# First layer of a selective-scan network: a new plan of the pieces in a round

## The chip, the cores and the metric

The kernel runs on one core of one Trainium2 chip. The metric is the device time of the whole kernel in microseconds; lower is better. A core has five engines that run at the same time, each with its own queue of instructions in a fixed order: TensorE (PE in the profile, matrix products; PEld its weight loads), VectorE (DVE), ScalarE (ACT), GpSimd (POOL) and SyncE (SP), which here issues almost all DMA transfers. An engine that reaches an instruction whose inputs aren't ready waits, and everything behind that instruction in its queue waits with it.

## The reference

Two layers work on an image x of 4 x 64 x 64 x 192. Only the first matters here. It normalizes x, projects it to 384 channels, and runs a selective scan over the 4096 positions in four directions k (by rows, by columns, and both backwards):

```python
delta = softplus(delta + delta_bias)          # one step size per channel and position
def step(h, inp):
    dt, ut, bt, ct = inp
    dA = exp(dt[..., None] * A_k[None])       # A has the 16 values -1 .. -16 for each channel
    dBu = dt[..., None] * bt[:, :, None, :] * ut[..., None]
    h = dA * h + dBu
    y = einsum('bkdn,bkn->bkd', h, ct)        # sum over the 16 states n
    return (h, y)
```

The four results are put back into image order and summed, normalized, gated, projected to 192 channels and added to x.

## The kernel before

The scan is not run position by position. `FirstLayer.scans` cuts the 4096 positions into 137 rounds of 30 positions. In a round the four directions and four images are handled together, with two blocks of positions on the 128 partitions, and the 16 states n are worked through one after another: a round is 16 **steps**, and step s of the program (`for s in range(-LEAD, N + 8)`, line 1094 on) belongs to round s // 16. The decays are exponentials of sums of dt inside the round, and since the sixteen values of A are whole multiples of one, the tile x of one state follows from the one before by one multiplication with a common factor f.

In every step, by its line in the profile:

- `grown` (L1073, on the first state of a round L1069) makes x for a later step: POOL multiplies 1024 of the 1536 columns, DVE the other 512. POOL is six steps ahead (`AHEAD = 6`), DVE five. On the first state DVE reads the exponentials that `first_near` (L916) put into the PSUM tile p.
- `carry_in` (L1024, two DMAs) puts the state that earlier rounds left into eight rows of x. It is issued three steps ahead of the use.
- `mix` (L1079) is the product on PE, in two halves j, each 8 matmuls into the accumulator accs[j] in PSUM. `weigh` (L1090, DVE, one for each half) multiplies the accumulator by fd; in the last step of a round `end_y` (L962) does so into the output tile y.
- In odd steps ACT copies the accumulators before they are weighed (`keep_end`, L1029, two halves). From that copy and from `decay` (L1039, ACT) and `settle` (L1042, POOL) comes the state for the next round, which SP moves (L1016 small, L1045 carry).
- In even steps PE makes the outer products of b and c for two later states (`outer`, L1053) and DVE cuts them out with a mask (`cut_b`, L1061).

Around this the preparation of the next rounds is threaded in pieces. `Round.steps` is a plan written out by hand: each entry is a step, counted from the round's first, an engine, and a piece. The pieces are: `v` (L845, a product on PE), `parts` (L862 and L863, ACT), `exp` (L867, ACT), `plus` (L871, ACT), `rounded` (L875, POOL), `log` (L878, ACT), eight `delta` products (L845, PE) that together give softplus, `times_u` (L890, DVE), `keep_dt` (L895, ACT); then sums of dt on PE, `sums_far` (L899), `sums_near` (L913) and `sums_d` (L845), and their exponentials on ACT: `first_far` and `fall_far` (L904, L909), `first_near` and `fall_near` (L916, L920), `keep_sums` (L929, which gives fd); and the sixteen `spread` pieces (L837, ACT), which make the weights of `outer`. All these products go through one single PSUM tile, p: a new product waits until the last reader of the one before is done. Three more `sums_d(0)` in the plan compute what nobody reads.

`keep_total` (DMA, L1016), `log_total` (L937, ACT) and `test` (L940, DVE) guard the range: `test` takes a running minimum into `far`, a corner of the second bank of accs[1], in columns that the products don't use.

Inside a step the program emits the work in the order of the loop: SP's, then ACT's copies, `decay`, the planned ACT pieces, POOL's, then DVE's `weigh`, `grown`, `cut_b`, the planned DVE pieces, then PE's `mix` for the next step, the planned PE pieces, and `outer`. Each engine keeps that order. Waits between engines are set by a tracker of tiles; nothing reorders.

Of the kernel before, what the change touches and what calls it, by code (L numbers as in the profile page):

```python
# [14 lines left out]
NB, HW, CH = 4, 64, 192  # L15
# [15 lines left out]
PART = 4  # L31
# [547 lines left out]
class FirstLayer(Stage):  # L579
# [182 lines left out]
    def scans(self):  # L762
        nc, tc = self.tc.nc, self.tc
        with ExitStack() as ctx:
            pool = lambda name, bufs, **k: ctx.enter_context(tc.tile_pool(name=name, bufs=bufs, **k))
# [43 lines left out]
            class Round:  # L809
# [164 lines left out]
                def steps(self):  # L974

                    s = lambda f, *a: (lambda: f(*a))
                    r = [(-30, "sp", self.load_xd), (-20, "sp", self.load_u), (-12, "sp", self.load_bc)]
                    for i in range(NS // PART):
                        r += [(PART * i - 8 + b, "act", s(self.spread, i, b)) for b in range(NB)]
                    for j in range(2):  # L980
                        r += [(2 * j - 21, "pe", s(self.v, j)), (2 * j - 20, "act", s(self.parts, j))]
                        r += [(2 * j - 19, "act", s(self.exp, j))]
                        r += [(2 * j - 13, "dve", s(self.times_u, j)), (2 * j - 13, "act", s(self.keep_dt, j))]
                        r += [(2 * j - 10, "pe", s(self.sums_d, j)), (2 * j - 9, "act", s(self.keep_sums, j))]
                    r += [(at, "pe", s(self.delta, 0, i)) for i, at in enumerate((-17, -16, -15, -14))]
                    r += [(at, "pe", s(self.delta, 1, i)) for i, at in enumerate((-13, -13, -12, -12))]
                    r += [(-16, "act", self.plus), (-15, "pool", self.rounded), (-14, "act", self.log)]
                    for i, at in ((1, -10), (2, -8)):
                        r += [(at - 1, "pe", s(self.sums_far, i))]
                        r += [(at, "act", s(self.first_far, i)), (at, "act", s(self.fall_far, i))]  # L990
                    r += [(-6, "pe", self.sums_near), (-5, "act", self.first_near), (-5, "act", self.fall_near)]
                    r += [(-4, "sp", self.keep_total), (-2, "act", self.log_total), (-1, "dve", self.test)]
                    r += [(10, "sp", self.load_y), (NS + 5, "pool", self.add_old), (NS + 6, "sp", self.store_y)]
                    r += [(at, "pe", s(self.sums_d, 0)) for at in (-7, -4, -2)]
                    return r

            w_dt, one, shift, zeros, late = self.w_dt, self.one, self.shift, self.zeros, self.late
# [2 lines left out]
            AHEAD = 6  # L1000
# [7 lines left out]
            def planned(s, engine):  # L1008
                for f in plan.get((s, engine), []):
                    f()  # L1010
# [7 lines left out]
            def carry_in(s):  # L1018
                n = state(s)
                m = (n - 1) // 2  # L1020
                v = carry[:, n % 2, m : m + 2].rearrange("c m q r f -> r (m q) c f")
                for r in range(2):
                    to = xs[s][r * HALF + 2 * RW : (r + 1) * HALF].rearrange("q (c f) -> q c f", c=2)
                    nc.sync.dma_start(to, v[r])  # L1024

            def keep_end(s, j):
                if j == 0:
                    sxs[s] = p3.tile([128, W], F32, name="sx")
                nc.scalar.copy(paired(sxs[s], j), accs[j][:, :, :DI])  # L1029

            def shrink(s):
                small[s] = p3.tile([128, SMALL], F32, name="small")
                for c in range(2):
                    narrow(small[s], sxs[s], c)

            def decay(s):
                back[s] = p3.tile([128, SMALL], F32, name="back")
                n = state(s)
                nc.scalar.activation(back[s], of(s).tot, AF.Exp, bias=late[:, n // 2 : n // 2 + 1], scale=float(n))  # L1039

            def settle(s):
                nc.gpsimd.tensor_tensor(back[s], back[s], small[s], ALU.mult)  # L1042

            def carry_out(s):
                nc.sync.dma_start(carry_of(carry, (state(s) - 1) // 2), back[s])  # L1045

            def outer(s):
                outs[s] = ps_o.tile([128, LC], F32, name="o")
                cs, p = of(s).cs[s % NS // PART], of(s).r % 2
                for h in range(2):  # L1050
                    n = state(s) - 1 - h
                    at = slice(h * NB * HALF, (h + 1) * NB * HALF)
                    nc.tensor.matmul(  # L1053
                        outs[s][:, at], at_b[p][:, n, :], cs[:, n % PART].rearrange("q b l -> q (b l)"),
                        start=True, stop=True, skip_group_check=True,
                    )

            def cut_b(s):
                bs[s] = p_b.tile([128, 2, NB, HALF], F32, name="b")
                o = outs[s].rearrange("p (h b l) -> p h b l", h=2, b=NB)  # L1060
                nc.vector.tensor_tensor(bs[s], o, bc(masks, 2, NB), ALU.mult)  # L1061

            def grown(s, engine):
                it = of(s)
                if s not in xs:
                    xs[s] = p_x.tile([128, W], F32, name="x")
                if s % NS == 0:
                    part, g = (slice(0, LC), it.m[:, 1, :]) if engine is nc.vector else (slice(LC, W), it.g)
                    engine.tensor_tensor(xs[s][:, part], it.dtu[:, part], g, ALU.mult)  # L1069
                    return  # L1070
                part = slice(0, LC) if engine is nc.vector else slice(LC, W)
                f = it.f0 if engine is nc.vector else it.f
                engine.tensor_tensor(xs[s][:, part], xs[s - 1][:, part], f, ALU.mult)  # L1073

            def mix(s, j):
                for r in range(2):
                    for c in range(2):
                        b = 2 * c + j
                        nc.tensor.matmul(  # L1079
                            accs[j][half(c), r, :DI], bs[s - s % 2][half(r), s % 2, b, :], xs[s][half(r), cols(b)],  # L1080
                            start=s % NS == 0, stop=state(s) == 1, skip_group_check=True,
                        )

            def weigh(s, j):
                n = state(s)
                if n == 1:
                    of(s).end_y(j)
                    return
                acc = accs[j][:, :, :DI]
                nc.vector.tensor_tensor(acc, acc, paired(of(s).fd, j), ALU.mult)  # L1090

            engines = {e.engine for e in (nc.tensor, nc.scalar, nc.vector, nc.gpsimd, nc.sync)}
            with tc.manual_schedule(engines=engines):
                tc.keep_in_program_order(nc.scalar.preload_act_table_set("natural_log_exp_and_others"))
                for s in range(-LEAD, N + 8):
                    on = lambda q: 0 <= q < N
                    pair = lambda q: on(q) and state(q) % 2 == 1
                    if pair(s - 1):
                        shrink(s - 1)
                    if pair(s - 5):  # L1100
                        carry_out(s - 5)
                    if on(s + AHEAD - 3):
                        carry_in(s + AHEAD - 3)
                    planned(s, "sp")
                    if pair(s):
                        for j in range(2):
                            keep_end(s, j)
                    if pair(s - 2):
                        decay(s - 2)
                    planned(s, "act")  # L1110
                    if on(s + AHEAD):
                        grown(s + AHEAD, nc.gpsimd)
                    if pair(s - 4):
                        settle(s - 4)
                    planned(s, "pool")
                    if on(s):
                        for j in range(2):
                            weigh(s, j)
                    if on(s + AHEAD - 1):
                        grown(s + AHEAD - 1, nc.vector)  # L1120
                    if on(s + 2) and s % 2 == 0:
                        cut_b(s + 2)
                    planned(s, "dve")
                    for j in range(2):
                        if on(s + 1):
                            mix(s + 1, j)
                    planned(s, "pe")
                    if on(s + 4) and s % 2 == 0:
                        outer(s + 4)
# [719 lines left out]
```

## Time and profile before

| what | us |
|---|---|
| median of 3 runs (9069.08 to 9072.87) | 9069.21 |
| the profiled execution, its own time | 9073.65 |
| its span | 9071.8 |
| scans of the first layer in it, about | 690 to 7320 |
| PE busy | 8250.5 (91%) |
| DVE busy | 7532.0 (83%) |
| POOL busy | 6608.1 (73%) |
| ACT busy | 6053.4 (67%) |

Times in the text are microseconds. A profile row of the timeline gives the start, the duration, the engine, the line, the operation, the tiles it writes and reads, the shape, and how many such instructions in a row were joined; in brackets stands how long the engine had idled before it and what ended that ("issue" where the profile shows no cause). DVE and ACT instructions overlap a little: a weighing lasts 0.96, but the next instruction starts 0.87 after it. A row of the waits gives who waited, for what, then the us in total, how many times, and the longest.

### The profile page before, as it was taken

What the parts mean: (1) busy time and instruction counts of PE and PEld (TensorE: products, weight loads), DVE (VectorE), ACT (ScalarE), POOL (GpSimd) and SP (SyncE); (2) the same over time, 40 slices, a digit from 0 to 9 for tenths busy, and PEclk for the clock granted to TensorE, in tenths of its full rate; (3) what the DMA queues carried; (4) which work ended last, traced back from release to release, by engine and by line L of the source; (5) the groups of instructions that cost most, each with busy time, mean ns of one, the idle gap of its engine ahead of it and who ended that gap; (6) DMA issues with size and microseconds to landing.
All of it is one profiled execution on the core that took longest, in us unless ns stands there. A gap on an engine that the chain in (4) does not pass through costs nothing. (4 is left out here: it accounts for less than half of the span.)

```text
span 9071.8 us, 194263 instructions
## 1 busy us (share of the span) xinstructions
PE 8250.5 (91%) x64280; PEld 3615.7 (40%) x64280; DVE 7532.0 (83%) x10238; ACT 6053.4 (67%) x10104; POOL 6608.1 (73%) x3814
## 2 busy tenths in 40 slices
PE   8989999999999999999999999999999945786668
PEld 4433333333333333333333333333333335443457
DVE  3328999999999999989999999999999954796756
ACT  3336777777777777766776777777677745575658
POOL 0008999999999999999999999999999942001460
PEclk9999999999999999999999999999999977887789
DMA  6652333323333333233333333333333379343558
GB/s 186 211 183 65 75 76 75 78 75 76 75 79 75 75 76 78 73 76 83 82 83 81 83 83 86 81 82 84 82 80 85 82 204 255 111 137 119 163 134 294
DMA packets 952264, 971.21 MB, mean 107 GB/s; under 512 B 550175, under 2 KB 802732, under 8 KB 950368
## 3 DMA queue, kind: packets, MB, share of 16 engines
q1 hardware_dynamic: 946192, 951.97, 38.6%
q0 software_dynamic: 5056, 6.66, 0.5%
q8 instruction: 519, 8.50, 0.4%
q14 instruction: 497, 4.07, 0.1%
HBM read 521.83 MB, written 375.80 MB: 99 GB/s over the span
## 5 line engine op out<-in xcount | busy, mean ns | idle before, releaser
L1073 POOL TENSOR_TENSOR x<-x,f 128x1024 f32<-128x1024 f32 x2055 | 4865.3, 2368 | 412.4 <-PE acc L1079 102.9
L1090 DVE TENSOR_TENSOR acc<-acc,fd 128x768 f32<-128x768 f32 x4110 | 3763.7, 959 | 272.2 <-ACT sx L1029 232.9
L1079 PE MATMUL acc<-x,b 64*64 64x384 f32 x35072 | 3502.3, 501 | 104.8 <-DVE acc L940 49.3
L1029 ACT COPY sx<-acc 128x768 f32<-128x768 f32 x2192 | 1669.0, 807 | 1011.9 <-PE acc L1079 910.5
L1079 PEld LDWEIGHTS acc<-x,b 64*64 64x64 f32 x35072 | 1075.1, 132 | 2100.3 <-DVE acc L1090 1577.0
L1073 DVE TENSOR_TENSOR x<-x,f 128x512 f32<-128x512 f32 x2055 | 1391.6, 677 | 0.1
L1053 PE MATMUL o<-cs,at_b 8*128 8x256 f32 x4384 | 1235.6, 400 | 2.4 <-DVE b L1061 2.4
L837 ACT ACTIVATE cs<-at_c,own 8x256 f32<-8x256 f32 x2192 | 1069.0, 494 | 2.8 <-PE o L1053 2.7
L1053 PEld LDWEIGHTS o<-cs,at_b 8*128 8x128 f32 x4384 | 726.9, 184 | 750.2 <-issue 269.3
L1061 DVE TENSOR_TENSOR b<-o,masks_f 128x512 f32<-128x512 f32 x1096 | 749.1, 683 | 4.7 <-PE o L1053 4.7
L462 PE MATMUL pp<-xT,w_in 96*128 96x512 f32 x1536 | 713.8, 616 | 20.9 <-ACT pad L1286 20.3
L875 POOL TENSOR_SCALAR d<-l 128x1536 f32<-128x1536 f32 x137 | 201.6, 1471 | 668.9 <-ACT l L871 668.9
L845 PE MATMUL p<-dt,steps_f 64*64 64x384 f32 x5480 | 598.1, 505 | 43.2 <-ACT up L863 25.5
L904 ACT ACTIVATE g<-p,shift 128x512 f32<-128x512 f32 x274 | 188.3, 687 | 492.7 <-PE p L899 492.7
L1300 DVE SCALAR_TENSOR_TENSOR acc<-pad,conv_w_s,acc 128x2048 f32<-128x2048 f32 x192 | 440.7, 2344 | 47.7 <-ACT acc L1298 46.4
L965 POOL TENSOR_TENSOR yt<-yt,yold 128x1536 f32<-128x1536 f32 x137 | 471.7, 3443 | 0.0
L462 PEld LDWEIGHTS pp<-xT,w_in 96*128 96x128 f32 x1536 | 291.9, 197 | 369.7 <-issue 340.9
L1042 POOL TENSOR_TENSOR back<-back,small 128x96 f32<-128x96 f32 x1096 | 424.3, 387 | 15.4 <-DMA small<-sx 6.4
L1039 ACT ACTIVATE back<-tot,late_f 128x96 f32<-128x96 f32 x1096 | 431.3, 394 | 0.0
L862 ACT ACTIVATE e<-p 128x768 f32<-128x768 f32 x274 | 221.5, 808 | 286.5 <-PE p L845 268.9
L549 PE MATMUL op<-w_out,v 128*128 128x192 f32 x1536 | 286.5, 344 | 132.2 <-DVE ot L552 96.4
L1281 POOL MEMSET pad<- 128x66 f32 x12 | 1.9, 158 | 554.5 <-DVE acc L1300 491.1
(218 smaller groups left out, 9650.9 us busy)
## 6 DMA issues: line engine op xcount, KB each, us to landing
x<-carry SPq DMA_DIRECT2D x4384, 24.0 KB
ut<-uT SPq DMA_DIRECT2D x548, 180.0 KB
small<-sx SPq DMA_DIRECT2D x2192, 24.0 KB
carry<-back SPq DMA_DIRECT2D x1096, 48.0 KB
zg<-gate SPq DMA_DIRECT2D x64, 768.0 KB
yold<-y_row SPq DMA_DIRECT2D x546, 90.0 KB
y_row<-yt SPq DMA_DIRECT2D x546, 90.0 KB
y_col<-yt SPq DMA_DIRECT2D x546, 90.0 KB
```

Of the source, the lines that this page charges most:

```text
L462: self.tc.nc.tensor.matmul(pp, self.w_in[:, i, e * 128 : (e + 1) * 128], self.xT[:, i, t * LC : (t + 1) * LC], start=(i == 0), stop=(i == ...
L837: nc.scalar.mul(self.cs[part][:, :, b, :], at_c[self.r % 2][:, at : at + PART, :], own[:, b : b + 1])
L845: nc.tensor.matmul(self.m[half(b), a, :DI], w(a, 2 * b + j), t(a, 2 * b + j), start=start and n == 0, stop=stop and n == len(terms) - 1, s ...
L965: nc.gpsimd.tensor_tensor(self.y, self.y, yold, ALU.add)
L1029: nc.scalar.copy(paired(sxs[s], j), accs[j][:, :, :DI])
L1039: nc.scalar.activation(back[s], of(s).tot, AF.Exp, bias=late[:, n // 2 : n // 2 + 1], scale=float(n))
L1053: nc.tensor.matmul(outs[s][:, at], at_b[p][:, n, :], cs[:, n % PART].rearrange("q b l -> q (b l)"), start=True, stop=True, skip_group_chec ...
L1061: nc.vector.tensor_tensor(bs[s], o, bc(masks, 2, NB), ALU.mult)
L1073: engine.tensor_tensor(xs[s][:, part], xs[s - 1][:, part], f, ALU.mult)
L1079: nc.tensor.matmul(accs[j][half(c), r, :DI], bs[s - s % 2][half(r), s % 2, b, :], xs[s][half(r), cols(b)], start=s % NS == 0, stop=state(s ...
L1090: nc.vector.tensor_tensor(acc, acc, paired(of(s).fd, j), ALU.mult)
L1300: nc.vector.scalar_tensor_tensor(acc, part(tap), weight(tap), acc, ALU.mult, ALU.add)
```

## The change

The entries of the plan get other steps. `v`, `parts`, `exp`, `plus`, `rounded` and `log` move one step earlier. The sums are reordered: `sums_d` now in steps 5 and 7 of the round before (counted 0 to 15), `sums_far` in steps 6 and 8, `sums_near` in step 9. Their ACT pieces follow: `keep_sums` in steps 6 and 8, `first_far` and `fall_far` in steps 7 and 9, `first_near` and `fall_near` in step 10. The spreads go in pairs into even steps. The three unread products move to steps 11, 13 and 14.

In the loop, `carry_in` is issued four steps ahead instead of three; DVE's `grown` is six steps ahead like POOL's; the planned ACT pieces come before `decay`; and `test` has a place of its own, ahead of the step's `weigh` and `end_y`.

```diff
                     for i in range(NS // PART):
-                        r += [(PART * i - 8 + b, "act", s(self.spread, i, b)) for b in range(NB)]
+                        r += [(PART * i - 8 + b // 2 * 2, "act", s(self.spread, i, b)) for b in range(NB)]
                     for j in range(2):
-                        r += [(2 * j - 21, "pe", s(self.v, j)), (2 * j - 20, "act", s(self.parts, j))]
-                        r += [(2 * j - 19, "act", s(self.exp, j))]
+                        r += [(2 * j - 22, "pe", s(self.v, j)), (2 * j - 21, "act", s(self.parts, j))]
+                        r += [(2 * j - 20, "act", s(self.exp, j))]
                         r += [(2 * j - 13, "dve", s(self.times_u, j)), (2 * j - 13, "act", s(self.keep_dt, j))]
-                        r += [(2 * j - 10, "pe", s(self.sums_d, j)), (2 * j - 9, "act", s(self.keep_sums, j))]
+                        r += [(2 * j - 11, "pe", s(self.sums_d, j)), (2 * j - 10, "act", s(self.keep_sums, j))]
+                        r += [(2 * j - 10, "pe", s(self.sums_far, j + 1))]
+                        r += [(2 * j - 9, "act", s(f, j + 1)) for f in (self.first_far, self.fall_far)]
...
-                    r += [(-16, "act", self.plus), (-15, "pool", self.rounded), (-14, "act", self.log)]
-                    for i, at in ((1, -10), (2, -8)):
-                        r += [(at - 1, "pe", s(self.sums_far, i))]
-                        r += [(at, "act", s(self.first_far, i)), (at, "act", s(self.fall_far, i))]
-                    r += [(-6, "pe", self.sums_near), (-5, "act", self.first_near), (-5, "act", self.fall_near)]
-                    r += [(-4, "sp", self.keep_total), (-2, "act", self.log_total), (-1, "dve", self.test)]
+                    r += [(-17, "act", self.plus), (-16, "pool", self.rounded), (-15, "act", self.log)]
+                    r += [(-7, "pe", self.sums_near), (-6, "act", self.first_near), (-6, "act", self.fall_near)]
+                    r += [(-4, "sp", self.keep_total), (-2, "act", self.log_total), (-1, "sum", self.test)]
...
-                    r += [(at, "pe", s(self.sums_d, 0)) for at in (-7, -4, -2)]
+                    r += [(at, "pe", s(self.sums_d, 0)) for at in (-5, -3, -2)]
...
-                    if on(s + AHEAD - 3):
-                        carry_in(s + AHEAD - 3)
+                    if on(s + AHEAD - 2):
+                        carry_in(s + AHEAD - 2)
                     planned(s, "sp")
                     if pair(s):
                         for j in range(2):
                             keep_end(s, j)
+                    planned(s, "act")
                     if pair(s - 2):
                         decay(s - 2)
-                    planned(s, "act")
...
                     planned(s, "pool")
+                    planned(s, "sum")
                     if on(s):
                         for j in range(2):
                             weigh(s, j)
-                    if on(s + AHEAD - 1):
-                        grown(s + AHEAD - 1, nc.vector)
+                    if on(s + AHEAD):
+                        grown(s + AHEAD, nc.vector)
```

## The prediction

> **What bounds the kernel now.** First the page's 40 slices and two stretches, to find the stage; then the timeline of one clean round, engine by engine; then the waits.
>
> ```profile
> span 9071.8 us, 194263 instructions
> PE   8989999999999999999999999999999945786668
> DVE  3328999999999999989999999999999954796756
> POOL 0008999999999999999999999999999942001460
> ```
>
> ```profile
> 690.00:7320.00 6630.00, 6409.77 (x56622) 2467.34 (x56618) 6124.69 (x8085) 4703.91 (x8066) 6189.72 (x3565) 0.99 0.32 79
> 2338.33:2385.93 47.60, 46.51 (x414) 17.62 (x414) 44.66 (x60) 34.42 (x60) 45.18 (x26) 1.00 0.31 76
> ```
>
> (Columns: length, then busy us of PE, weight loads, DVE, ACT, POOL; granted clock.) The change touches the scans alone: 6630 of 9072 us, 137 rounds of 16 steps. The second row is one clean round of 47.60: PE 46.5, POOL 45.2, DVE 44.7. Three engines are nearly full, so no single one is "the" bound; a round is lost in small waits between them. From the first L962 (758.2) to the last (7306.0) lie 136 rounds, 48.1 each: besides the clean 47.6 there is about 0.55 of disturbance.
>
> ```profile
> 2359.85 1.83 DVE L1090 TENSOR_TENSOR acc<-acc,fd 128x768 f32<-128x768 f32 x2 [0.41 <-ACT sx L1029]
> 2365.69 1.83 DVE L1090 TENSOR_TENSOR acc<-acc,fd 128x768 f32<-128x768 f32 x2 [0.49 <-ACT sx L1029]
> 2373.62 0.69 DVE L1069 TENSOR_TENSOR x<-dtu,p 128x512 f32<-128x512 f32 x1 [0.85 <-issue]
> 2377.54 1.83 DVE L1090 TENSOR_TENSOR acc<-acc,fd 128x768 f32<-128x768 f32 x2 [0.30 <-ACT sx L1029]
> 2383.43 1.82 DVE L962 TENSOR_TENSOR yt<-acc,fd 128x768 f32<-128x768 f32 x2 [0.55 <-ACT sx L1029]
> 2385.77 0.26 DVE L940 TENSOR_TENSOR acc<-acc,tot 128x96 f32<-128x96 f32 x1
> ```
>
> These are steps 7, 9, 11, 13, 15: DVE waits for ACT's copies (L1029) or for ACT's exponentials. Packed, DVE repeats at 0.87 (weighing), 0.60 (growth), 0.60 (cut), 0.17 (test): 44.0 a round, so 3.6 are waits. ACT and PE, same round:
>
> ```profile
> 2364.29 0.68 ACT L909 ACTIVATE f<-p,shift 128x512 f32<-128x512 f32 x1
> 2364.86 1.50 ACT L1029 COPY sx<-acc 128x768 f32<-128x768 f32 x2
> 2372.87 0.66 ACT L920 ACTIVATE f<-p,shift 128x512 f32<-128x512 f32 x1
> ```
>
> ```profile
> 2362.54 1.12 PE L899 MATMUL p<-dt,steps_f 128*128 128x512 f32 x2
> 2363.59 1.52 PE L1079 MATMUL acc<-x,b 64*64 64x384 f32 x16
> 2365.02 0.88 PE L845 MATMUL p<-dt,steps_f 64*64 64x384 f32 x8
> 2365.82 1.12 PE L1053 MATMUL o<-cs,at_b 8*128 8x256 f32 x4
> 2366.88 1.57 PE L1079 MATMUL acc<-x,b 64*64 64x384 f32 x16
> 2386.08 0.88 PE L1079 MATMUL acc<-x,b 64*64 64x384 f32 x8 [0.58 <-DVE acc L940]
> ```
>
> The copies of step 9 stand right behind L909; PE runs without a gap from 2362.54 to 2366.88. Its pitches: both products 1.43, L845 0.80, L899 or L913 1.05, L1053 1.06.
>
> ```profile
> PEld acc L1079 <- DVE acc L940: 135.9, 135, 1.3
> ACT tot L937 <- DMA tot<-fd: 79.8, 70, 2.4
> PE acc L1079 <- DMA x<-carry: 41.4, 71, 6.4
> ```
>
> **Steps of the reckoning.** From the timeline: first weighing to the next step's product 1.03 (2371.0 to 2372.0 and alike); product to copy 0.89, copy to weighing 0.84, product to weighing without a copy 0.95; L899's start to its exponential 1.16. I lay the changed plan out with these, in us after the round's first weighing (before: read off):
>
> start of step 2, 5, 6, 8, 10, 11, 12, 14, next 0
> before: 5.56, 14.89, 18.09, 23.85, 29.69, 32.62, 35.89, 41.54, 47.60
> after: 5.34, 14.68, 17.87, 23.60, 29.43, 33.69, 36.04, 41.59, 47.81
>
> How the second row comes: step 1's second product starts at 0.87 + 1.03 = 1.90, then delta and L1053 end at 4.40, + 0.94 = 5.34. Step 5: two delta products wait for times_u (start 10.60, + 0.95 + 0.06), 1.34 long, then 0.89 + 0.84. Step 6: + 3.19, DVE packed with times_u. Step 8 and 11: (a), (b). Step 10: step 9's second product at 25.59, + 0.78 + 1.06 + 1.05 = 28.48, + 0.95. Step 12: v(0) at 33.23, + 0.80 + 1.06 + 0.95. Step 14: step 13's second product at 38.03, + 0.75 + 0.80 + 1.06 + 0.95. Next 0: L962 at 45.48 (d), + 0.87 + 0.86 + 0.60.
>
> **Part by part.**
> (a) *Far exponentials to odd steps, sums between.* Step 6 now gives ACT only keep_sums (0.78) ahead of the copies, not two of 0.59 behind a longer product. The 0.49 at step 7 goes (17.87 + 2.93 = 20.80). But L899 (1.05) now shares the even step with L1053 (1.06): the second product of step 7 starts at 19.77, + 0.75 + 1.05 + 1.06 = 22.65 before step 8's product may start, + 0.95 = 23.60 where DVE would be ready at 23.13. The same again at step 10. What ACT gives, PE's queue takes: steps 6 to 10 last 11.56 against 11.60. Gain 0.04.
> (b) *Near sums, and DVE's growth one step earlier.* L1069 waited for L920, not merely for L916, which it reads: it starts 0.09 after L920's end (2373.53), 1.06 after L916's. Now L913 follows step 10's products: 28.48 + 1.43 = 29.91; L916 at +1.16, L920 +0.66, L1069 at 32.48. DVE is ready at 29.43 + 1.73 = 31.17: 1.31 lost against 0.85-0.95 before, because L1069 moved forward as well. Behind it stand the cut and step 11's weighing; on PE, v(0) waits for the buffer and L1053 behind v(0). Steps 10 to 12: 6.61 against 6.20, loss 0.41.
> (c) *v, parts, exp one step earlier.* In step 14 ACT keeps exp (0.73) instead of parts (1.40), in step 12 exp instead of parts: the 0.30 at step 13 nearly goes, PE holds back 0.1 and 0.19. Steps 12 to 14: 5.55 against 5.65, gain 0.10. Plus (1.45, ahead of a decay) falls into step 15 behind copies, with 2 us till the next; rounded then fills POOL's idle time at the round's start. No cost; without that cover, 1.45.
> (d) *Test ahead of the products of y.* The test writes accs[1]. L940 held step 0's second product, though that product touches other columns (0.58 above); that goes. But in front of L962 the test must wait for what reads accs[1] before it: the second copy. Page "PSUM — Partial Sum Buffer", section "PSUM bank collisions raise a hardware error": guard by bank and quadrant, not by address. By addresses the test would cost 0.17, and the round end at 47.02; by the rule it waits until 44.47 + 0.84 = 45.31 and L962 starts at 45.48, not 44.69: 0.79. The row (products held by a test in other columns) sides with the rule, so I take 0.79. Behind the test stand both L962, the growth, step 0's weighing; PE's products and so POOL wait for these. Step 14 to the following round's step 1: 9.15 against 9.27, gain 0.12, where (c) alone would have brought 0.6.
> (e) Steps 0 to 6 otherwise: loss 0.06 (step 1 without its former slack, step 4 to 5 as before: the two delta products behind times_u).
> Sum: +0.04 +0.10 +0.12 -0.41 -0.06 = -0.21 a round, 29 us slower in 137.
> (f) *Spreads in pairs*: as many, in even steps, where ACT idles; 0. Decay behind the planned work: settle on POOL reads it two steps later; 0 to 0.1. The spare products stay three; the clock stays 1.00.
> (g) *Carry transfers a step earlier.* 32 DMAs a round pass, in SP's queue, the loads and stores of their step: y stores (8 of about 0.42, step 6), y loads (step 10). Product 11, which waits for them, is later in about a fourth of the rounds: in the mean of all rounds step 10 lasts 0.28 more than in a clean one (weighing starts, timeline). One step is 3 us, and (b)'s stall covers 1 us more: I take it all, -0.28; at least nothing, as the transfer also waits for growth, POOL's included, one step nearer.
> (h) *Late totals* (second half; y loads are then twice as many): step 14 and 15 last 0.25 and 0.26 more there. The first stays (exp, copies and test stand behind L937 as parts did). The second goes: the spare product of step 14 no longer waits for parts. Over all rounds -0.13, at least 0.
> Together +0.21 - 0.28 - 0.13 = -0.20 a round, 27 us. The profiled run is 9073.65 against a median of 9069.2; the difference is taken off the median: about **9043**.
>
> **Rivals.**
> 1. *Gains add up* (0.12): the test doesn't wait for the copies, or PE's queue yields in (a). For: every DVE wait of the timeline names ACT, which is relieved. Against: rows above. With the test free -0.79 more: 9043 - 108 = **8935**.
> 2. *SP's queue takes it back* (0.28), the slower side. Carry_in now needs POOL's growth of the step before. In step 7 that ends at 2359.7 (after add_old), DVE's at 2358.9: SP is held 0.8, with the small transfers, y loads and totals behind. In the second half SP issues almost without a pause, so the 0.8 reaches L937, the copies and the test: nothing of (g) and (h) is saved and 67 rounds pay 0.8 more: 9069 + 29 + 54, less 41 (carry waits on PE, row above) if these go: 9111 to 9152; I take **9111**. It decides where totals land more than 1.2 us after step 14's weighing.
>
> **How the numbers follow.** Likeliest 0.60, range of its own 9005 to 9085 (0.25 a round either way for ten pitches of 0.05 to 0.1 uncertainty, and (g), (h) half or whole). About 0.2% (18 us) is what a measurement tells. Faster: 0.33 of the likeliest, 0.12 of rival 1: 0.45. Within: 0.22 + 0.04: 0.26. Slower: 0.05 + 0.24: 0.29. The range reaches half-way to rival 1 and to the near end of rival 2: 8965 to 9112.
>
> **What would show it.** (a) Step 6 to 7 at 2.93, and step 7 to 8 up from 2.33 to about 2.8 with no gap on PE. (b) L1069 with 1.3 idle ahead, L920 its releaser. (c) no wait at step 13. (d) the test idle until the second copy, L940 gone from PE's waits. (g) x<-carry gone from PE's waits. A clean round near 47.8. Wrong if a clean round is under 47.3 or L940 doesn't wait; wrong the other way if SP's wait for POOL at L1024 grows by tens of us.

## The result and the profile after

Side by side the changed kernel takes 9054.55 (median of 12 runs, 9027.24 to 9067.12) against 9075.01 (12 runs, 9055.05 to 9096.4): ratio 0.9973, 95% interval 0.9961 to 0.9984, a gain of about a quarter of a per cent. Applied to the 9069.21 of the table above this is 9045, beside a forecast of 9043. The time came out as forecast, but some terms of the sum did not; they offset each other.

In the changed kernel all lines of the loop are one lower (weighing L1089, products L1078, growth L1068 and L1072, cut L1060, L1052 for L1053, copies L1028, carry_in L1023); L940, L962, L913 to L937 keep their numbers.

The whole scan stage, a clean round and a longer one, in the columns used above:

```profile
690.00:7300.00 6610.00, 6360.42 (x56619) 2481.66 (x56618) 6109.44 (x8085) 4846.18 (x8069) 6192.73 (x3565) 0.99 0.32 79
2335.70:2383.36 47.66, 46.16 (x422) 18.01 (x418) 44.57 (x61) 35.48 (x60) 45.18 (x27) 1.00 0.31 77
2383.36:2432.40 49.04, 47.54 (x422) 18.64 (x418) 44.82 (x61) 35.31 (x59) 45.16 (x27) 0.97 0.30 75
```

The clean round is 47.66: not shorter than the 47.60 of before. The next has the same instructions, lasts 1.38 more, and its granted clock is 0.97. DVE in the clean round, the rows around the waits that changed:

```profile
2359.30 1.83 DVE L1089 TENSOR_TENSOR acc<-acc,fd 128x768 f32<-128x768 f32 x2 [0.40 <-PE acc L1078]
2365.04 1.83 DVE L1089 TENSOR_TENSOR acc<-acc,fd 128x768 f32<-128x768 f32 x2 [0.41 <-PE acc L1078]
2368.16 0.69 DVE L1068 TENSOR_TENSOR x<-dtu,p 128x512 f32<-128x512 f32 x1 [1.28 <-issue]
2377.20 1.83 DVE L1089 TENSOR_TENSOR acc<-acc,fd 128x768 f32<-128x768 f32 x2 [0.15 <-PE acc L1078]
2380.86 0.27 DVE L940 TENSOR_TENSOR acc<-acc,tot 128x96 f32<-128x96 f32 x1 [0.64 <-ACT sx L1028]
2381.03 1.81 DVE L962 TENSOR_TENSOR yt<-acc,fd 128x768 f32<-128x768 f32 x2
```

By their starts these are steps 8, 10 (two rows), 14 and 15 (two rows). DVE's waits for ACT in steps 7, 9 and 13 are gone; in steps 8, 10 and 14 it waits for PE instead. The growth at L1068 waits 1.28 instead of 0.85; the test, now ahead of L962, waits for a copy. ACT and PE around the growth:

```profile
2366.71 0.66 ACT L916 ACTIVATE p<-p,shift 128x512 f32<-128x512 f32 x1 [1.25 <-PE p L913]
2367.41 0.66 ACT L920 ACTIVATE f<-p,shift 128x512 f32<-128x512 f32 x1
```

```profile
2356.24 1.12 PE L899 MATMUL p<-dt,steps_f 128*128 128x512 f32 x2
2357.30 1.13 PE L1052 MATMUL o<-cs,at_b 8*128 8x256 f32 x4
2358.35 1.52 PE L1078 MATMUL acc<-x,b 64*64 64x384 f32 x16
2365.55 1.13 PE L913 MATMUL p<-dt,steps_f 128*128 128x512 f32 x2
2368.90 0.87 PE L845 MATMUL p<-w_dtk_f,xd 26*64 26x384 f32 x8 [0.78 <-DVE x L1068]
2382.03 1.74 PE L1078 MATMUL acc<-x,b 64*64 64x384 f32 x16 [0.37 <-DVE yt L962]
```

L899 and L1052 stand back to back between the products of steps 7 and 8, and PE has no gap there: that is (a). L916 ends at 2367.37, but the growth that reads it starts at 2368.16, 0.09 after L920's end: that is (b), and PE's v(0) (L845) waits 0.78 for it. The last row is the product of the next round's step 0. Last, the waits:

```profile
DVE acc L940 <- ACT sx L1028: 100.5, 136, 7.5
PE p L845 <- DVE x L1068: 106.5, 136, 2.2
PE acc L1078 <- DVE yt L962: 62.6, 136, 5.7
ACT tot L937 <- DMA tot<-fd: 24.0, 26, 7.4
POOL x L1072 <- DMA x<-carry: 27.2, 33, 1.1
```

PE's wait for x<-carry (41.4 before) is gone, and so is its wait for L940 (135.9 of weight loads and 49.3 of products before). But the second of these has only moved on: ahead of step 0's product PE now waits for L962, 62.6 in all where it was 3.2 before, and L962 stands behind the test. ACT's wait for totals fell from 79.8 to 24.0.

**The account of a round.** Clean lengths are medians over the rounds, from weighing start to weighing start in the timeline:

| step | 0 | 1 | 2 | 3 | 4 | 5 | 6 | 7 | 8 | 9 | 10 | 11 | 12 | 13 | 14 | 15 | clean | mean |
|---|---|---|---|---|---|---|---|---|---|---|---|---|---|---|---|---|---|---|
| before | 3.21 | 2.35 | 2.93 | 3.19 | 3.20 | 3.20 | 3.42 | 2.33 | 3.51 | 2.33 | 2.93 | 3.28 | 3.32 | 2.33 | 3.56 | 2.50 | 47.60 | 48.18 |
| after | 2.93 | 2.40 | 2.93 | 3.19 | 3.20 | 3.20 | 2.93 | 2.81 | 2.93 | 2.81 | 4.32 | 2.34 | 2.93 | 2.56 | 3.83 | 2.32 | 47.65 | 48.03 |

The mean of all rounds fell by 0.15, the clean one rose by 0.05. What fell is the excess of the mean over the clean length: before, step 10 had 0.28, steps 14 and 15 had 0.13 each; after, step 10 has 0 and step 15 has 0, step 14 keeps 0.10. New are 0.09 at step 11 and 0.13 at step 12. Over 137 rounds -0.15 is 21 us, against 20 measured.

The 0.22 at steps 11 and 12 is the clock. The longer round above in three stretches:

```profile
2412.50:2416.00 3.50, 3.28 (x30) 0.91 (x22) 2.02 (x3) 2.22 (x5) 3.42 (x2) 1.00 0.32 80
2416.00:2419.50 3.50, 2.95 (x20) 1.35 (x24) 3.42 (x5) 3.15 (x6) 3.02 (x3) 0.81 0.37 105
2419.50:2423.00 3.50, 3.50 (x36) 1.38 (x32) 2.44 (x4) 1.34 (x4) 1.37 (x1) 0.71 0.29 63
```

and PE's rows in it:

```profile
2416.55 0.87 PE L845 MATMUL p<-w_dtk_f,xd 26*64 26x384 f32 x8 [0.77 <-DVE x L1068]
2418.62 2.84 PE L1078 MATMUL acc<-x,b 64*64 64x384 f32 x16
```

After the 0.77 of idle time before v(0) the product takes 2.84 instead of 1.52: about half the clock. The clock records of the trace show stretches at one half, each of 3.4 us (some of 6.8). In the scans before there are 10 (9 of them begin in step 15), after 25 (19 begin in step 11). Such a round costs 1.39 more, the rest is as in a clean round; 19 of 136 rounds by 1.39 is 0.19.

Which rounds are hit can be read from the same records. In each run all changes of the clock inside the scans lie on one grid of 3.413 us, to within 0.005; the grid runs on without regard to the rounds. In the changed kernel 19 of the gaps before v(0) began between 0.31 before a point of this grid and 1.12 after it: 18 of them were followed by half clock, and none of the other 114. With the test free (next section) it is 72 of 72, and none of 61. So where a gap falls in the grid decides. A clean round of 47.66 is 13.96 intervals: the gap creeps through the grid by 0.04 a round, and a hit, whose round is 49.04, throws it on by 0.37. By this estimate about one round in eleven is hit; it was one in seven.

### The profile page after: what moved, and what is told of

Read it like the earlier page. It is cut to its first block, busy times and chain, and to the rows that moved or that the text cites. A ratio compares the mean times of both kernels' runs of the same rounds, so it can differ in the third digit from the quotient of the medians.

```text
span 9055.1 us, 193788 instructions
## 1 busy us (share of the span) xinstructions
PE 8209.4 (91%) x64280; PEld 3630.8 (40%) x64280; DVE 7520.8 (83%) x10238; ACT 6193.2 (68%) x10104; POOL 6605.8 (73%) x3814
## 3 DMA queue, kind: packets, MB, share of 16 engines
q0 software_dynamic: 5056, 6.66, 0.6%
## 5 line engine op out<-in xcount | busy, mean ns | idle before, releaser
L1072 POOL TENSOR_TENSOR x<-x,f 128x1024 f32<-128x1024 f32 x2055 | 4865.9, 2368 | 323.0 <-issue 102.9
L1089 DVE TENSOR_TENSOR acc<-acc,fd 128x768 f32<-128x768 f32 x4110 | 3751.4, 958 | 195.2 <-PE acc L1078 151.4
L1078 PE MATMUL acc<-x,b 64*64 64x384 f32 x35072 | 3552.2, 502 | 69.2 <-DVE yt L962 62.6
L1028 ACT COPY sx<-acc 128x768 f32<-128x768 f32 x2192 | 1712.8, 800 | 1072.5 <-PE acc L1078 1032.2
L1078 PEld LDWEIGHTS acc<-x,b 64*64 64x64 f32 x35072 | 1056.2, 132 | 2084.6 <-DVE acc L1089 1397.3
L1072 DVE TENSOR_TENSOR x<-x,f 128x512 f32<-128x512 f32 x2055 | 1387.0, 675 | 0.1
L1052 PE MATMUL o<-cs,at_b 8*128 8x256 f32 x4384 | 1238.0, 401 | 3.7 <-DVE b L1060 3.5
L1052 PEld LDWEIGHTS o<-cs,at_b 8*128 8x128 f32 x4384 | 727.0, 184 | 772.4 <-DVE b L1060 363.1
L837 ACT ACTIVATE cs<-at_c,own 8x256 f32<-8x256 f32 x2192 | 979.8, 494 | 3.5 <-PE o L1052 3.5
L1060 DVE TENSOR_TENSOR b<-o,masks_f 128x512 f32<-128x512 f32 x1096 | 746.7, 681 | 5.7 <-PE o L1052 5.7
L845 PE MATMUL p<-dt,steps_f 64*64 64x384 f32 x5480 | 580.0, 493 | 5.0 <-DVE dtu L890 1.9
L929 ACT ACTIVATE fd<-p,shift 128x768 f32<-128x768 f32 x274 | 246.7, 900 | 300.2 <-PE p L845 300.2
L1038 ACT ACTIVATE back<-tot,late_f 128x96 f32<-128x96 f32 x1096 | 409.6, 374 | 0.0
L1068 POOL TENSOR_TENSOR x<-dtu,g 128x1024 f32<-128x1024 f32 x137 | 324.4, 2368 | 80.2 <-ACT g L904 77.6
```

The lines of the kernel that those rows point to most:

```text
L837: nc.scalar.mul(self.cs[part][:, :, b, :], at_c[self.r % 2][:, at : at + PART, :], own[:, b : b + 1])
L845: nc.tensor.matmul(self.m[half(b), a, :DI], w(a, 2 * b + j), t(a, 2 * b + j), start=start and n == 0, stop=stop and n == len(terms) - 1, s ...
L1052: nc.tensor.matmul(outs[s][:, at], at_b[p][:, n, :], cs[:, n % PART].rearrange("q b l -> q (b l)"), start=True, stop=True, skip_group_chec ...
L1078: nc.tensor.matmul(accs[j][half(c), r, :DI], bs[s - s % 2][half(r), s % 2, b, :], xs[s][half(r), cols(b)], start=s % NS == 0, stop=state(s ...
```

## The experiments

All ratios are to the kernel before on the same chip, with 95% intervals. The theory to be tried: the clean round is made of (b) and (d), the gain of (g) and (h), and PE's new idle time costs clock. Rivals are named with each run.

**The test made free.** The far total goes into an SBUF tile of its own, so that the test no longer writes accs[1]:

```diff
-            far = accs[1][:, 1, DI : DI + SMALL]
+            far = self.far
...
-            nc.vector.tensor_copy(self.far, far)
```

> The changed kernel, with the running minimum far in a tile of its own in SBUF instead of a corner of accs[1]; the copy of far at the end falls away. Theory (the test waits for the second copy only because it shares the accumulator's tile): the test costs its length, L962 starts when its own copy is there, about 0.7 sooner; PE's outer product then holds step 0's product a little. A clean round of 47.0 against 47.65, 89 us less than the changed kernel, ratio to the kernel before about 0.988 (0.985 to 0.991). Rival (the copies bound step 15, the test only hides in their shadow): a clean round stays at 47.65, ratio 0.997.

Measured: 9038.65 against 9080.56, 0.9947 (0.9932 to 0.9961). The test's row and two rounds of this kernel:

```profile
2237.08 0.30 DVE L940 TENSOR_TENSOR far_f<-far_f,tot 128x96 f32<-128x96 f32 x1
```

```profile
2192.65:2239.63 46.98, 45.85 (x422) 18.03 (x418) 44.53 (x61) 35.48 (x60) 45.15 (x27) 1.00 0.31 77
2239.63:2288.06 48.43, 47.30 (x422) 18.76 (x418) 44.80 (x61) 35.32 (x60) 45.15 (x27) 0.96 0.30 76
```

No bracket stands behind the test now: it does not wait. The clean round is 46.98, 0.67 shorter: the test's wait is what (d) costs. But against the changed kernel the time gains only 0.26%, where 0.67 a round over 137 rounds would be 1.0%, because rounds of 46.98 alternate with rounds of 48.4 at a clock of 0.96: 74 half-clock stretches, 71 of them beginning in step 11. The mean round is 47.87, 0.16 less than in the changed kernel. The part on the test holds, the expected time does not, and the clock is the reason. That there are 71 stretches and not 19 is no matter of PE's idle time: the gap before v(0) is as long as in the changed kernel, and a clean round has 1.13 of idle PE (46.98 less 45.85) against 1.50 (47.66 less 46.16). It is how the round fits the grid: 46.98 is 13.76 intervals and 48.43 is 14.19, so the gap falls in and out of the 1.4 us that are hit about every second round.

**The test put back**, at the end of DVE's step, with all else of the change kept:

```diff
-                    r += [(-4, "sp", self.keep_total), (-2, "act", self.log_total), (-1, "sum", self.test)]
+                    r += [(-4, "sp", self.keep_total), (-2, "act", self.log_total), (-1, "dve", self.test)]
```

> The changed kernel with the test alone put back behind the products of y. Theory (ahead of them it costs a wait for the second copy, behind them only a later second product of step 0): step 14 falls from 3.83 to about 3.05, step 15 and 0 get 0.2 and 0.2 longer: a clean round of 47.2 against 47.65, ratio to the kernel before about 0.991 (0.988 to 0.994), so faster than the changed kernel. Rival (the test ahead of the products is what made the change faster): slower than the changed kernel, ratio 1.000 or more.

Measured: 9052.58, 0.9968 (0.9955 to 0.998). The clean round is 47.16: moving the test costs 0.49 of the clean round. Here too the time does not follow: 69 stretches, mean round 48.02, the same time as the changed kernel, where a ratio of 0.991 was expected.

**The test moved alone**, in the kernel before:

```diff
-(-1, "dve", self.test)
+(-1, "sum", self.test)
...
                     planned(s, "pool")
+                    planned(s, "sum")
```

> The kernel before with nothing but the test put ahead of the products of y. Theory: L962 waits for the second copy, 0.7 to 0.9 later; the second product of step 0 no longer waits for the test, 0.25 back; a clean round of about 48.1 against 47.6, ratio 1.008 (1.004 to 1.012). Rival (only L940 leaves PE's waits): a clean round of 47.35, ratio 0.995.

Measured: 9146.87, 1.007 (1.0058 to 1.0082), clean round 48.07, step 14 up from 3.56 to 4.44.

```profile
2165.62 0.27 DVE L940 TENSOR_TENSOR acc<-acc,tot 128x96 f32<-128x96 f32 x1 [1.25 <-ACT sx L1029]
2165.80 1.81 DVE L962 TENSOR_TENSOR yt<-acc,fd 128x768 f32<-128x768 f32 x2
```

DVE stands 1.25 ahead of the test, with L962 right behind it. By itself this part loses 0.7%; in the changed kernel, with exp in place of parts ahead of step 14's copies, the wait is the 0.64 seen above. These three runs settle (d): the test waits for the copies though these read other columns of accs[1].

**The near growth freed from L920**, by writing L916's result to an SBUF tile:

```diff
-                    nc.scalar.activation(self.m[:, 1, :], self.m[:, 0, :], AF.Exp, bias=shift[-NS], scale=float(NS))
+                    self.g0 = p1.tile([128, LC], F32, name="g0")
+                    nc.scalar.activation(self.g0, self.m[:, 0, :], AF.Exp, bias=shift[-NS], scale=float(NS))
...
-                    part, g = (slice(0, LC), it.m[:, 1, :]) if engine is nc.vector else (slice(LC, W), it.g)
+                    part, g = (slice(0, LC), it.g0) if engine is nc.vector else (slice(LC, W), it.g)
```

> The changed kernel with the result of first_near in a tile of its own in SBUF instead of the second bank of p, which DVE's first growth reads there. Theory (that growth waits for fall_near only because both touch the tile p, and v(0) on PE waits for the growth): L1069 starts right behind first_near, its idle time falls from 1.39 to about 0.7, and v(0) starts right behind fall_near, 0.7 sooner; steps 10 and 11 together shorten by 0.7: a clean round of 46.9 to 47.0, ratio about 0.988 (0.985 to 0.991). Rival (PE is full, so what DVE gains there is lost in the steps that follow): a clean round of 47.4 or more, ratio 0.993 or above.

Measured: 9191.24, 1.0116 (1.0102 to 1.0131), slower where a gain was expected.

```profile
2558.73 1.78 DVE L1069 TENSOR_TENSOR x<-dtu,g 128x512 f32<-128x512 f32 x1 [0.62 <-issue]
```

```profile
2561.26 1.10 PE L1053 MATMUL o<-cs,at_b 8*128 8x256 f32 x4 [1.09 <-DVE b L1061]
```

The wait fell from 1.28 to 0.62, as the theory had it: the growth waited for L920 because L920 still read the PSUM tile in which L916's result lay (it read the other half of it). But the instruction now takes 1.78 instead of 0.69, so the cut behind it is later and PE waits 1.09 at L1053; the clean round is 48.05 and there are 90 stretches. DVE's two inputs now both lie in SBUF while POOL multiplies from SBUF. The Trainium skill, page "SBUF — State Buffer", section "Who interferes with whom", says that such an instruction contends with a GpSimd instruction that reads SBUF; this run agrees, with 1.1 us on 0.69. So the cure was refuted and the cause kept.

**The carries issued one step later again:**

```diff
-                    if on(s + AHEAD - 2):
-                        carry_in(s + AHEAD - 2)
+                    if on(s + AHEAD - 3):
+                        carry_in(s + AHEAD - 3)
```

> The changed kernel with carry_in alone put back to three steps ahead. Theory (the earlier issue takes the carry transfers out of PE's waits): waits of PE for x<-carry come back, between 10 and 40 us of them, and the scans get 5 to 25 us longer: ratio to the kernel before 0.998 to 1.000. Rival (SP pays for the earlier issue with waits for POOL's growth): faster than the changed kernel, ratio 0.995 or less, and SP's waits for DVE and POOL at L1023 shrink.

Measured: 9077.51 against 9077.93, 1.0001 (0.999 to 1.0012). The clean round stays 47.65; the mean is 48.24 instead of 48.03, and a row of before is back:

```profile
PE acc L1078 <- DMA x<-carry: 35.9, 38, 4.2
```

0.21 a round is 29 us, of the order of the whole gain: without the longer lead the change gains nothing that can be measured. It was expected a little below 1; the rival, that the carries cost as much as they bring, falls. But the 0.21 does not lie where (g) put it. In step 10, which lasted 0.28 more than a clean one before the change, only 0.05 comes back (6 waits of PE for x<-carry, 7.8 us). Of the other waits 25, with 25.6 us, stand ahead of step 0's product, all in the second half: step 15 is 0.08 longer than in the changed kernel and step 0 by 0.11, with 12 half-clock stretches that begin in step 15 instead of 4. SP's price for the longer lead shows in its own waits of the changed kernel:

```profile
SPq L1023 <- DVE x L1072: 243.4, 260, 5.5
```

(166.0 before): SP is held 77 us more by the growth, yet no wait of PE, DVE or ACT for a transfer grew.

**PE's and DVE's wait in step 10 filled**, by order alone: in that step the cut goes ahead of the growth, and L1052 ahead of v(0).

```diff
+                    first = s % NS == NS - AHEAD
+                    if on(s + 2) and first:
+                        cut_b(s + 2)
...
+                    if on(s + 4) and first:
+                        outer(s + 4)
```

> The changed kernel with two orders turned round in step 10 of every round: DVE cuts b before it waits for fall_near, and PE makes the outer product before v(0), so both engines work while they otherwise stand still. Theory (the wait for fall_near costs 1.3 to 1.4 on DVE and, through v(0), about 0.7 on PE; the clock drops at step 11 because PE stands still there): steps 10 and 11 together shorten by 0.6, a clean round of 47.0 against 47.65, and half-clock stretches at step 11 fall from 19 to fewer than 5: ratio about 0.987 (0.984 to 0.990). Rival (the half-clock stretches come from the sum of PE's idle time, wherever it lies): a clean round of 47.0, but stretches in 50 rounds or more as in the run with the test free, ratio 0.993 or above.

Measured: 8975.34 against 9077.93, 0.9889 (0.9872 to 0.9906).

```profile
2201.77 0.68 DVE L1060 TENSOR_TENSOR b<-o,masks_f 128x512 f32<-128x512 f32 x1
2203.15 0.69 DVE L1068 TENSOR_TENSOR x<-dtu,p 128x512 f32<-128x512 f32 x1 [0.69 <-issue]
```

```profile
2203.05 1.12 PE L1052 MATMUL o<-cs,at_b 8*128 8x256 f32 x4
2204.10 0.88 PE L845 MATMUL p<-w_dtk_f,xd 26*64 26x384 f32 x8
```

The cut covers half of DVE's 1.28, and PE has no gap before L845. Step 10 falls from 4.32 to 3.79, the clean round to 47.10, and no stretch begins in step 11 any more (14 in all, 12 of them in step 15); the mean is 47.48. So order alone brings back 0.55 of the clean round, more than (b)'s loss, and the stretches of step 11 belonged to PE's 0.78.

**Both, filled and the test free:**

```diff
+                    if on(s + 2) and first:
+                        cut_b(s + 2)
...
-            far = accs[1][:, 1, DI : DI + SMALL]
+            far = self.far
```

> Both: step 10 with the two orders turned round, and far in a tile of its own in SBUF. Theory: 47.65 less 0.6 less 0.67 is a clean round of 46.4, PE (about 45.8 packed) close to full, few half-clock stretches: ratio about 0.980 (0.976 to 0.984), faster than all so far. Rival (PE's idle time wherever it lies): stretches in 50 rounds or more, ratio 0.988 or above.

Measured: 8912.05 against 9077.93, 0.981 (0.9793 to 0.9828). Clean round 46.42, mean 47.03, 15 stretches, none from step 11. This is faster than both kernels by more than 1.5%. The second half is left with

```profile
ACT tot L937 <- DMA tot<-fd: 97.9, 68, 7.2
```

68 waits, about one for each round of it; step 14 lasts 0.86 more there than a clean one.

**The changed kernel without its three spare products:**

```diff
-                    r += [(at, "pe", s(self.sums_d, 0)) for at in (-5, -3, -2)]
```

> The changed kernel without the three spare products, which nobody reads. Theory (they keep PE's clock up): PE has 2.4 less to do in a round and a clean round falls by 0.1 to 0.3, but half-clock stretches come in far more rounds than 25, at 1.4 each: slower than the changed kernel, ratio 1.000 to 1.010. Rival (they only take PE's time): ratio 0.994 to 0.996, stretches as before.

Measured: 9162.1, 1.0099 (1.0081 to 1.0116). The clean round stays 47.65, not the 0.1 to 0.3 shorter that I had expected of it; but there are 131 stretches (73 from step 11, 51 from step 15), and the mean is 48.82.

```profile
690.00:7300.00 6610.00, 6219.88 (x52725) 2384.05 (x52723) 6049.90 (x7978) 4794.45 (x7983) 6119.43 (x3521) 0.96 0.31 78
```

A granted clock of 0.96 over all the scans, against 0.99. Products that nobody reads are worth 1.3% here (1.0099 against 0.9973): without them PE is 141 us less busy in the scans and the clock is lower.

**The totals asked for three steps earlier**, on top of the filled version with the free test:

```diff
-                    r += [(-4, "sp", self.keep_total), (-2, "act", self.log_total), (-1, "sum", self.test)]
+                    r += [(-7, "sp", self.keep_total), (-2, "act", self.log_total), (-1, "sum", self.test)]
```

> The kernel of e7 with keep_total three steps earlier (step 9 instead of 12, ahead of the y loads in SP's queue). Theory (the 0.43 that step 14 still loses in the mean there is ACT waiting for the totals, which land late behind the y loads: 97.9 of such waits): L937's waits for tot<-fd fall under 10, step 14 loses under 0.1, the mean round comes to 46.6: 45 to 60 less than e7, ratio to the kernel before about 0.976 (0.973 to 0.979). Rival (SP is simply behind, so something else in its queue is late instead, or the half-clock stretches are the cause and not the effect): the waits move to small or carry transfers, ratio 0.980 or more.

Measured: 8907.91 against 9066.0, 0.9815 (0.9799 to 0.983), no different from the version it stands on, where 0.976 was expected. ACT's wait for totals is gone, and in its place stands

```profile
PE acc L1078 <- DMA x<-carry: 38.6, 42, 2.0
```

which was 2.2 without it. The wait only passed to the next transfer (in the mean of all rounds step 14 lost 0.43 and now 0.02, step 0 lost 0.14 and now 0.45), as if SP's queue as a whole were behind in the second half.

**Fewer loads in the second half.** This kernel leaves out a part: there, it does not add the earlier results of the two column directions to y, and so does not load them (4 DMAs a round less).

```diff
-                    elif k % 2 == 0 or r >= MIDDLE:
+                    elif k % 2 == 0:
```

> The kernel of e7 without the four y loads a round that the second half of the rounds has more than the first: it leaves out part of the computation, the earlier results of the two column directions are not added in the second half. Theory (in the second half SP's queue is the bound: 90 transfers a round at about half a microsecond each, and whatever stands behind the y loads is late): the second half runs like the first, L937's waits for the totals fall under 15, the mean round comes to about 46.6 from 47.03, 50 to 70 less than e7, ratio to the kernel before about 0.974 (0.971 to 0.977). Rival (something else of the second half, such as the traffic in memory of the y stores): as e7, ratio 0.979 or more.

Measured: 8839.81 against 9061.03, 0.9758 (0.9739 to 0.9776). Nine rounds in ten lie within 46.42 to 46.44, the mean is 46.48, and one stretch is left. Against the version with them this is 0.55 a round over all rounds. Most of the second half, first with these loads, then without:

```profile
4000.00:7100.00 3100.00, 3034.94 (x27015) 1178.25 (x27012) 2931.27 (x3853) 2298.82 (x3852) 2952.62 (x1700) 0.99 0.34 84
4000.00:7100.00 3100.00, 3040.91 (x27316) 1180.01 (x27308) 2952.74 (x3909) 2328.32 (x3889) 2985.41 (x1722) 1.00 0.32 79
```

The work on POOL and DVE is about the same in a round (what lies in the buffer is added), and the 16 DMA engines are busy a third of the time in both (0.34 and 0.32, the column before the last), so it points to the issue of these loads on SP, ahead of totals and carries; transfer time by itself was not taken apart from issue time.

## Why the prediction was right, and where it was not

Each step's clean length stands in the account of a round; the forecast is that of the table of starts.

(a) Right. Steps 6 to 9 take 11.48, forecast 11.56, against 11.59 before: a gain of 0.11 instead of 0.04. PE's queue, without a gap, takes most of what ACT gives, 0.07 less than reckoned. This is seen in the trace alone; no run took it apart.

(b) Right, in mechanism and size. L1068 waits for L920, 1.28 idle where 1.31 was forecast; steps 10 and 11 take 6.66, forecast 6.61, against 6.21: a loss of 0.45 instead of 0.41. The run with L916's result in SBUF shows the cause (the shared PSUM tile), the filled run that the order behind it decides what it costs. What (b) costs in clock was left out; see (f).

(c) Right. Step 13's wait (0.30) is gone, and in step 14 DVE waits 0.15 for PE; steps 12 and 13 take 5.49, forecast 5.55, against 5.65: a gain of 0.16 instead of 0.10.

(d) Right, and the step on which most hung. The wait ahead of the test is 0.64 (forecast 0.79); freeing the test shortens the round by 0.67. Steps 14 to 0 take 9.08, forecast 9.15, against 9.27: a gain of 0.19 instead of 0.12. The prediction held that without the test's move this would be 0.48 more (0.6 for 0.12); the run with the test put back gives 0.49. The rule that was weighed there (the Trainium skill, page "PSUM — Partial Sum Buffer", section "PSUM bank collisions raise a hardware error": guard by bank and quadrant, not by address) decided rightly against the rival by addresses, under which the test would not have waited. That the guard goes by bank and not by the whole tile is not shown: in (b) L1068 waits for L920 though the two read different halves of p.

(e) Right: steps 1 to 5 lose 0.05, forecast 0.06.

The clean round so comes to +0.05 instead of +0.21: three gains of (a), (c) and (d) were each sized 0.06 or 0.07 too low, (b)'s loss 0.04 too low.

(f) **Failed.** "The spare products stay three; the clock stays 1.00." The first half is true; the second does not follow from it. The prediction had v(0) on PE wait for the growth in (b), and costed that wait for the queue behind it, not for the clock. In the trace of before, v(0) followed the products without a gap; now PE stands 0.78 there in every round, 19 stretches of half clock begin there, and that costs 0.22 a round. The filled run takes the gap away and with it the stretches of step 11. The size of 0.22 is in part chance, since it hangs on how the round fits the grid.

(g) Right in size, only partly in cause. Step 10's 0.28 went to 0, but with late carries just 0.05 of it comes back there. So something else in the change took most of it; the prediction named (b)'s stall as a second cover, which no run tried alone. The lead earns the rest of its 0.21 at the end of the round and in clock, where the prediction gave it nothing.

(h) Right in size: step 15's 0.13 went, step 14's stayed (0.10). That the spare product of step 14 alone took it is not shown: before, PE also waited in step 15 for x<-carry, 15.9 us in all, and with late carries 0.08 of the 0.13 comes back. (g) and (h) together hold; their split does not.

In sum +0.05 - 0.28 - 0.13 + 0.22 = -0.14, near the forecast -0.20: the clean term was 0.16 too high, and the clock's 0.22 was missing. Both errors are as large as the result; that they offset is luck. (The prediction's own -0.20 is 27 us, so 9042 by its rule and not 9043.)

Rival 1 (gains add up) needed a free test: with it the clean round is 46.98, but the time, put on the 9069 of the table, is 9021 and not 8935, for the most part because of the clock. Rival 2 (SP's queue takes it back) failed: SP waits for POOL's growth at L1023 15.3 us in all the scans, and the gain of (g) is there. Its premise, that SP's queue is the limit of the second half, fits the last two runs all the same, once the waits of the clean round are smaller.

Open: how long a gap must be, or which share of busy time, to halve the clock. Which of the gaps of 0.78 do so is settled by the grid; why a gap in the other 2.0 us of an interval does not is open. Nor was (a) tried by itself, and no run parts the longer lead from (b)'s stall in step 10.

## To carry to other kernels

Where three engines are nearly full, taking work from one moves its wait to the queue of the next; look for the wait that replaces it, and fill it by the order of work that doesn't depend on it (here worth 0.8% on the changed kernel, with the freed test 1.6%). When a change leaves PE idle even for 0.8 us, read the granted clock by round before you cost it: a shorter clean round can be paid back there in full, and how often it is hit changes with the round's length. And a transfer's lead is worth a term of its own: here one line that issues it earlier made about the whole gain of the change.

## What was not expected of the hardware

- PE was busy for 3.28 and then 2.95 of 3.50 us, with one gap of 0.77, and the clock went to one half for about 3.4 us. Whether such a gap does it was decided by where it fell in a grid of 3.413 us (18 of 19 in one part of it, none of 114 in the rest). The Trainium skill, page "TensorE: Matmul & The Clock Gate", section "HAM oscillation — how this bites in real kernels", warns of gaps in PE's work of more than some 3.4 us; here gaps a quarter as long did it, and filling them ended the stretches of step 11. The measurement decides.
- Work that nobody reads can shorten the time: 25 stretches with three spare products a round, 131 without, 1.3% of the time.
- Two instructions on ACT and DVE that read different halves of one PSUM tile did not run at once: L1068 began 0.09 after L920's end in nearly every round. The tracker of tiles sets the program's waits; whether the chip would need this one, no run shows.
- A 128x512 multiplication on DVE took 1.78 with both inputs in SBUF and 0.69 with one in PSUM, while POOL worked.
